# Candidates of two statistics in one four-bank PSUM tile, and paired VectorE word steps, in a four-layer graph kernel on one Trainium2 core

## The chip, the core and the metric

The kernel runs on one core of a Trainium2 chip. The metric is device time in microseconds for one execution of the whole program. In this text PE is TensorE (its weight loads are PEld), DVE is VectorE, ACT is ScalarE, POOL is GpSimd and SP is the engine that issues most transfers. L1151 is line 1151 of the kernel.

## The reference

Inputs are `x` (16 batches, 1024 nodes, 64 channels), a symmetric 0/1 matrix `adj` (16, 1024, 1024) with some 6% ones, and a node mask. Four layers follow one another, each as `x = x + layer(h)` with `h = max(layernorm(x), 0)`. Layer 0 is the costly one and the one that is changed. It takes, for every node and every channel, three quantiles over the node's neighbours, after some neighbours have been dropped:

```python
vals = jnp.where(nd[..., None], x[:, None, :, :], jnp.inf)     # nd: kept neighbours
s = jnp.sort(vals, axis=2)
nv = nd.sum(2)
for tau, w in zip((0.25, 0.5, 0.75), (0.25, 0.5, 0.25)):
    pos = tau * max(nv - 1, 0)
    lo, hi, frac = floor(pos), ceil(pos), pos - floor(pos)
    agg = agg + w * (v_lo + frac * (v_hi - v_lo))              # s at lo and at hi
out = x + agg
y = relu(out @ W1 + b1) @ W2 + b2
```

Layers 1 to 3 are a gated message passing, a small tanh network on `adj @ h`, and an attention with a softmax over columns; each multiplies a 1024x1024 matrix by node features.

## The kernel before

**No sort by neighbour list.** The kernel sorts each channel once over all 1024 nodes and then finds each node's quantiles by counting. `sort_pair` sorts the 128 channel rows of two batches at a time with a network of 55 compare steps on DVE. Forward, a step is three instructions: the comparison (L729, kept in DRAM as a mask), the maximum (L736) and the minimum (L737); each step needs the one before. Backward, the masks are loaded again and the positions are carried back through the same steps (L753, L754, then L760, or L756 and L757), which gives every node its rank as a code of a word (11 ranks) and a bit within it.

**Counting by matmul.** `neighbours` builds the kept-neighbour matrix `ndT` of a batch (scans on DVE at L825, transposes and sums on PE). `weights` turns codes into fp8 one-hot words, `wt`. `select` then handles one batch in four groups of two 128-node tiles (`TG = 2`), with these parts for each group:

- `words`: matmuls of `ndT` with `wt` (L1043) into PSUM tiles `comb` (four banks, four tiles), whose results ACT writes as 16-bit words `y` (L1051). PE transposes them (L1096) and ACT makes the sign matrices `sign` from them (L1098).
- `lasts`: on DVE, a tree of maxima over `y` (L1109, L1114, L1116 to L1125) that leaves in `z`, for each channel, the word in which the wanted rank lies. `y` has 36 rows of words, 32 called `full` and 4 called `rest`.
- `places`: some 26 16-bit bit operations on `z` (L966, L968, L971), which give four masks that say at which of the 12 lanes of the word the wanted value lies: `f2`, `f1`, `f`, `e0`.
- `values`: matmuls of `sign` with a table of value differences `vtab` (L1143) give, for every channel, the 12 candidate values of the word. Four copies under the four masks (L1151) move the wanted lane to lane 11, and `add_to` (L1018 the first time, L1020 after) adds it, times a coefficient, to `agg`.

There are two statistics (the median, and the two outer quantiles together, index `n`) and two signs (`sec`), so four candidates tiles for each 128-node tile, each `[P, 2, 512]` in two banks with channels halved over `e`. The pool `sc` has two buffers, so four banks; `comb` has the other four. The matmuls of one statistic number 40 (`n` = 0) or 32 (`n` = 1).

**Order.** Batches go in eight pairs. For a pair, `select` runs twice (with `compact` for rare nodes that need another way), then `extras` for those rare nodes of both batches (L1251 to L1317, with its own calls of `places` and of `pick`, the latter at L1011), then `layers` for both, up to the last addition at L1530. The neighbours and the sort of later pairs stand in the same part of the source, but a tile framework with a list scheduler writes the order on each engine: instructions without dependence are moved in between, by its own estimates, within what pools and buffers allow. So DVE's sort steps of the next pair fill places in `select`, `extras` and `layers` of the current one. Each engine then works strictly in that order and waits on semaphores.

```python
for i in range(2):
    wt, positive = weights(pr * 2 + i, kn, None if i else taken)
    select(pr * 2 + i, i, wt, positive, *made[i], aggs[i], kept, sw, sg, sy, sc, sp)
taken = extras(pr, kept, aggs, xs, xp)
for i, (ly, lb) in enumerate(((ly0, lb0), (ly1, lb1))):
    layers(pr * 2 + i, (pr * 2 + i) % 4, aggs[i], ly, lb)
if pr + 1 < pairs:
    made = prepare(pr + 1, nb, nbp)
    sort_pair(pr + 1, cur, sop)
```

Of the kernel before, what the change touches and what calls it, by code (L numbers as in the profile page):

```python
# [9 lines left out]
F32 = mybir.dt.float32  # L10
# [13 lines left out]
P = 128  # L24
# [18 lines left out]
def gnn_stack(ctx, tc, x, adj, nodemask, w, out):  # L43
# [915 lines left out]
    def places(sw, z, nf, kept=2):  # L959

        def word(name, bufs=1):
            return sw.tile([P, nf], U16, name=name, bufs=bufs)

        def bits(dst, src, v0, o0, v1=None, o1=None):
            if v1 is None:
                nc.vector.tensor_single_scalar(dst, src, v0, op=o0)  # L966
            else:
                nc.vector.tensor_scalar(dst, src, v0, v1, op0=o0, op1=o1)  # L968

        def both(dst, p, q, op):  # L970
            nc.vector.tensor_tensor(dst, p, q, op=op)  # L971

        zf = z.rearrange("p t s c -> p (t s c)")
        m, r, a, s0, s1, u1, u2 = (word(f"w_{n}") for n in ("m", "r", "a", "s0", "s1", "u1", "u2"))
        f1, f2, f, e0 = (word(f"w_{n}", kept) for n in ("f1", "f2", "f", "e0"))
        bits(m, zf, 1, SHL, 0xFFE, AND)
        bits(r, zf, 11, SHR, 31, XOR)
        bits(s0, m, 1, SHR, 0x555, AND)
        both(a, m, s0, ALU.subtract)
        bits(s0, a, 2, SHR, 0x333, AND)  # L980
        bits(s1, a, 0x333, AND)
        both(s1, s0, s1, ALU.add)
        bits(s0, s1, 8, SHR)
        bits(s1, s1, 4, SHR, 15, AND)
        both(s1, s1, s0, ALU.add)
        both(u1.bitcast(I16), r, s0, ALU.subtract)
        both(u2.bitcast(I16), r, s1, ALU.subtract)
        both(r, r, u1, ALU.min)
        both(r, r, u2, ALU.min)
        bits(f1, u1, 13, SHR, 4, AND)  # L990
        bits(f2, u2, 13, SHR, 4, AND)
        both(s0, f1, f2, ALU.add)
        both(m, m, s0, SHR)
        both(a, a, s0, SHR)
        bits(s1, a, 2, SHR, 3, AND)
        both(u1.bitcast(I16), r, s1, ALU.subtract)
        both(r, r, u1, ALU.min)
        bits(f, u1, 14, SHR, 2, AND)
        both(m, m, f, SHR)
        bits(s0, m, 1, SHR, 1, AND)  # L1000
        both(e0, s0, r, ALU.is_gt)
        return [v.rearrange("p (t s c) -> p t s c", t=z.shape[1], s=z.shape[2]) for v in (f2, f1, f, e0)]
# [13 lines left out]
    def add_to(ag, first, v, c):  # L1016
        if first:
            nc.vector.tensor_scalar(ag, v, c, None, op0=ALU.mult)  # L1018
        else:
            nc.vector.scalar_tensor_tensor(ag, v, c, ag, op0=ALU.mult, op1=ALU.add)  # L1020
# [7 lines left out]
    def select(b, i, wt, positive, ndT, row10, qb, qz, agg, kept, sw, sg, sy, sc, sp):  # L1028
        coef = row10[:, :, 3:9].rearrange("p t (k s) -> p t k s", s=2)
        if True:  # L1030
# [74 lines left out]
            def lasts(ys):  # L1105

                z = sw.tile([P, TG, 4, C], U16, name="z", bufs=2)
                for tl, y in enumerate(ys):
                    nc.vector.tensor_scalar_add(y[:, 1], y[:, 0], 2048.0)  # L1109

                    yu = y.bitcast(U16)
                    full, rest = yu[:, :, : 2 * NQ], yu[:, :, 2 * NQ :]
                    for v, n in ((full, 64), (full, 32), (full, 16), (full, 8), (rest, 64), (rest, 32), (rest, 16)):
                        nc.vector.tensor_tensor(v[:, :, :, :n], v[:, :, :, :n], v[:, :, :, n : 2 * n], op=ALU.max)  # L1114
                    zs = z[:, tl].rearrange("p (s k) c -> p s k c", k=2)
                    nc.vector.tensor_tensor(  # L1116
                        zs[:, :, 1, :].rearrange("p s (q d) -> p s q d", d=4), full[:, :, NQ:, :4], full[:, :, NQ:, 4:8],
                        op=ALU.max,
                    )
                    nc.vector.tensor_tensor(full[:, :, :NQ, :4], full[:, :, :NQ, :4], full[:, :, :NQ, 4:8], op=ALU.max)  # L1120
                    for s in range(2):
                        nc.vector.tensor_tensor(
                            zs[:, s, 0, :].rearrange("p (m q d) -> p m q d", m=4, d=4),
                            full[:, s, :NQ, :4].rearrange("p (m q) d -> p m q d", m=4),
                            rest[:, s, :, :16].rearrange("p m (q d) -> p m q d", d=4), op=ALU.max,  # L1125
                        )
                return z

            def values(g, signs, marks):
                for tl in range(TG):  # L1130
                    t = g * TG + tl
                    for s in range(4):
                        sec, n = divmod(s, 2)
                        cand = sc.tile([P, 2, 512], F32, name="cand")
                        for e in range(2):

                            terms = [(n * NQ + q, n, q, 4, (q % 8) * 48) for q in range(8 * e, 8 * e + 8)]
                            if n == 0:
                                terms += [(2 * NQ + m, 2, m, 16, (m % 2) * 192) for m in range(2 * e, 2 * e + 2)]
                            for i_, (chunk, part, q, d_, at) in enumerate(terms):  # L1140
                                tab = vtab[:, part].rearrange("p (q d l) -> p q d l", d=d_, l=24)
                                for half_ in range(2):
                                    nc.tensor.matmul(  # L1143
                                        cand[:, e, at : at + 12 * d_].rearrange("p (d l) -> p d l", l=12),
                                        signs[tl][sec][:, chunk, :], tab[:, q, :, half_ * 12 : half_ * 12 + 12],
                                        start=(i_ == 0 and half_ == 0), stop=(i_ == len(terms) - 1 and half_ == 1),
                                    )
                        v = cand[:, :, :384].rearrange("p e (c l) -> p e c l", l=12)
                        for (dst, frm, k), mk in zip(PICKS[1:], marks):
                            mk = mk[:, tl, s, :].rearrange("p (e c o) -> p e c o", e=2, o=1)  # L1150
                            nc.vector.copy_predicated(  # L1151
                                v[:, :, :, dst : dst + k], mk.to_broadcast([P, 2, C // 2, k]), v[:, :, :, frm : frm + k]
                            )
                        add_to(
                            agg[:, t, :].rearrange("p (e c) -> p e c", e=2), s == 0, v[:, :, :, 11],
                            coef[:, t, STATS[n], sec : sec + 1],
                        )

            nf = TG * 4 * C
            now = words(0)  # L1160
# [405 lines left out]
    for pr in range(pairs):  # L1566
        with tc.tile_pool(reuse_waits="tile", name="keep", bufs=1) as keep:
# [5 lines left out]
            with tc.tile_pool(reuse_waits="tile", name="kn", bufs=1) as kn:  # L1573
                with (
# [1 line left out]
                    tc.tile_pool(reuse_waits="tile", name="sw", bufs=1) as sw,  # L1576
                    tc.tile_pool(reuse_waits="tile", name="sg", bufs=2) as sg,
                    tc.tile_pool(reuse_waits="tile", name="sp", bufs=4, space=PSUM) as sp,
                    tc.tile_pool(reuse_waits="tile", name="sc", bufs=2, space=PSUM) as sc,
                ):  # L1580
                    for i in range(2):
                        wt, positive = weights(pr * 2 + i, kn, None if i else taken)
# [66 lines left out]
```

## Time and profile before

| | |
|---|---|
| three runs | 5937.49, 5952.29, 5957.01 us (median 5952.29) |
| the profiled execution | 5945.84 us, of which the span of its instructions is 5944.1 |
| mean granted TensorE clock | 0.838 |
| DVE busy | 5122.3 us (86%), 13031 instructions |
| PE busy | 4397.4 us (74%), 45010 matmuls |
| ACT busy | 3817.2 us (64%) |
| `values` matmuls, L1143 | 669.3 us |
| `values` copies, L1151 | 2048 instructions; the groups of 256, 128 and 64 elements took 420.1, 150.3 and 108.6 us |
| tree, L1114 | 672.1 us, 896 instructions |

A group's row gives busy time, the mean time of one instruction, and the idle time of its engine just before it with what ended that. Consecutive instructions of DVE overlap in these durations, so the sum of durations is more than the time they take. All shares are over the whole span, which has stages with different limits.

### The profile page before, as it was taken

The page shows a single profiled execution, that of the slowest core. Times are in us where ns is not written, and L with a number is a line of the kernel's source. Part 1 is how long each engine was busy: PE and PEld are TensorE (multiplying, and loading weights), DVE is VectorE, ACT ScalarE, POOL GpSimd, SP SyncE. Part 2 cuts the span into 40 slices and gives each one's busy share as a digit, 9 for nine tenths or more (in the row PEclk, how much of TensorE's full clock was granted, in tenths as well). Part 3 has the DMA queues.
Part 4 walks back from the last instruction along what each step waited for, and adds up shares of the span by engine and source line. Part 5 has one row for each costly group of instructions (what it writes and reads, how often), then busy time and mean ns, then how long its engine had stood idle before and what let it go on. Part 6 is the DMA issues. An engine that isn't in the chain of part 4 may idle for free. (4 is left out here: it accounts for less than half of the span.)

```text
span 5944.1 us, 114264 instructions
## 1 busy us (share of the span) xinstructions
PE 4397.4 (74%) x45010; PEld 2736.4 (46%) x45010; DVE 5122.3 (86%) x13031; ACT 3817.2 (64%) x5701; POOL 181.7 (3%) x283
## 2 busy tenths in 40 slices
PE   1488677895768858788577885788767886779856
PEld 1355443554435544355434554345443554436542
DVE  9999888998789987999879997798879999567744
ACT  2587647775576855668567665676566776577824
POOL 2000000000000000000000000000000000000000
PEclk5699778997889978899688996899868998789967
DMA  3401364014631146211561115611345013520024
GB/s 126 123 26 37 97 200 127 30 48 120 194 94 34 38 127 212 77 36 44 152 204 55 50 51 150 190 39 48 90 141 172 34 48 97 183 87 19 10 75 139
DMA packets 524419, 568.22 MB, mean 96 GB/s; under 512 B 263808, under 2 KB 413568, under 8 KB 523872
## 3 DMA queue, kind: packets, MB, share of 16 engines
q1 hardware_dynamic: 381472, 476.43, 26.3%
q10 hardware_dynamic: 140064, 81.84, 4.5%
q8 instruction: 355, 5.82, 0.4%
q0 software_dynamic: 2336, 2.57, 0.2%
q14 instruction: 192, 1.57, 0.1%
HBM read 376.95 MB, written 183.76 MB: 94 GB/s over the span
## 5 line engine op out<-in xcount | busy, mean ns | idle before, releaser
L1043 PE MATMUL comb<-wt,ndT 128*128 128x512 fp8e5 x6144 | 1442.3, 387 | 146.7 <-ACT sign L1098 121.7
L1051 ACT ACTIVATE y<-comb,qb 128x512 int16<-128x512 f32 x1152 | 744.1, 718 | 512.4 <-PE comb L1043 510.7
L1043 PEld LDWEIGHTS <-ndT 128*128 128x128 fp8e5 x6144 | 592.5, 99 | 876.8 <-issue 246.3
L1143 PE MATMUL cand<-vtab,sign 128*128 128x48 f16 (+1 forms) x18432 | 669.3, 191 | 54.0 <-DVE agg L1018 36.1
L1143 PEld LDWEIGHTS <-sign 128*128 128x128 fp8e5 x18432 | 645.2, 96 | 111.9 <-issue 51.8
L1098 ACT ACTIVATE sign<-comb,lower 128x1024 fp8e5<-128x1024 int16 (+1 forms) x640 | 696.5, 1088 | 0.0
L1098 ACT ACTIVATE sign<-comb,half 128x1024 fp8e5<-128x1024 int16 (+1 forms) x640 | 691.3, 1080 | 0.0
L1114 DVE TENSOR_TENSOR y<-y 128x512 uint16<-128x512 uint16 (+5 forms) x896 | 672.1, 792 | 8.4 <-PE comb L1096 7.2
L1151 DVE COPY_PREDICATED cand<-w_f,cand 128x256 f32<-128x256 uint16 (+1 forms) x1536 | 535.8, 383 | 75.0 <-PE cand L1143 72.8
L1096 PE MATMUL comb<-ident_b,y 128*128 128x128 bf16 x4608 | 316.9, 222 | 117.2 <-ACT sign L1098 76.8
L833 ACT COPY at<-pk 128x512 f32<-128x512 f32 x256 | 147.5, 586 | 384.5 <-PE pk L831 197.1
L1406 PE MATMUL bank<-adjT,nd 128*64 128x512 f32 x1024 | 307.4, 668 | 90.4 <-DMA adjT<-a_d 88.9
L1096 PEld LDWEIGHTS <-y 128*128 128x128 bf16 x4608 | 292.7, 99 | 145.5 <-issue 144.4
L875 PE MATMUL pk<-minus_b,rem 128*128 128x128 bf16 x1024 | 225.5, 247 | 175.2 <-ACT rem L856 175.1
L1406 PE MATMUL bank<-att,hs 128*64 128x512 f32 x512 | 211.0, 941 | 185.0 <-ACT hs L1522 185.0
L825 DVE TENSOR_TENSOR_SCAN cum<-ni 128x1024 f16<-128x1024 fp8e5 x128 | 295.0, 2306 | 32.6 <-POOL ni L821 23.2
L875 PE MATMUL pk<-ident_b,ni 128*128 128x128 bf16 x1024 | 223.3, 244 | 125.1 <-ACT ndT L881 62.7
L729 DVE TENSOR_TENSOR swapped<-s 128x512 uint16<-128x512 f32 x440 | 302.5, 687 | 5.8 <-ACT s L717 1.6
L737 DVE TENSOR_TENSOR s<-s 128x512 f32<-128x512 f32 (+2 forms) x440 | 289.8, 659 | 0.0
L736 DVE TENSOR_TENSOR s<-s 128x512 f32<-128x512 f32 (+2 forms) x440 | 289.6, 658 | 0.0
L921 DVE TENSOR_SCALAR wt<-node 128x2048 uint8<-128x2048 f16 x224 | 268.0, 1221 | 13.1 <-PE comb L1234 13.0
L831 PE MATMUL pk<-ident,a 128*128 128x128 f32 x1024 | 193.5, 339 | 112.9 <-DMA a<-in_adj_dram 79.8
(323 smaller groups left out, 8258.8 us busy)
## 6 DMA issues: line engine op xcount, KB each, us to landing
adjT<-a_d SPq DMA_DIRECT2D x384, 512.0 KB
a<-in_adj_dram SPq DMA_DIRECT2D x128, 512.0 KB
a_d<-at ACTq DMA_DIRECT2D x256, 256.0 KB
m_d<-swapped SPq DMA_DIRECT2D x104, 512.0 KB
swapped<-m_d SPq DMA_DIRECT2D x104, 512.0 KB
n_d<-nat SPq DMA_DIRECT2D x128, 128.0 KB
x_d<-xr SPq DMA_DIRECT2D x48, 256.0 KB
comb_x<-x_d ACTq DMA_DIRECT2D x24, 512.0 KB
```

What stands on the lines that cost most here:

```text
L729: nc.vector.tensor_tensor(side(swapped[:, k, :], j), hi, lo, op=ALU.is_gt)
L737: nc.vector.tensor_tensor(to_hi, lo, hi, op=ALU.min)
L825: nc.vector.tensor_tensor_scan(cum[:, t - t0, :], ni[:, t, :], wide[:, t, pad - 1 : pad - 1 + N], 0.0, op0=ALU.add, op1=ALU.add)
L875: nc.tensor.matmul(pk[:, n % 4, :], lhs, rhs, start=(n % 4 == 0 and m == 0), stop=(m == len(terms) - 1 and last),)
L1043: nc.tensor.matmul(pw, ndT[:, j, t * P : (t + 1) * P], wt[1 + g8][:, j].rearrange("p w c -> p (w c)"), start=(j == 0), stop=(j == NT - 1),)
L1051: nc.scalar.activation(y[:, 0, chunks, at : at + 8 * d_].rearrange("p q (w d) -> p q w d", d=d_), pw.rearrange("p (w q d) -> p q w d", w=8 ...
L1096: nc.tensor.transpose(pt[:, q - q0, :], y[:, 0, q, :].bitcast(BF16), ident_b)
L1098: nc.scalar.activation(signs[tl][s][:, q0:q1, :], pt.bitcast(I16), AF.Sign, bias=before[s], scale=-1.0, saturate=False,)
L1114: nc.vector.tensor_tensor(v[:, :, :, :n], v[:, :, :, :n], v[:, :, :, n : 2 * n], op=ALU.max)
L1143: nc.tensor.matmul(cand[:, e, at : at + 12 * d_].rearrange("p (d l) -> p d l", l=12), signs[tl][sec][:, chunk, :], tab[:, q, :, half_ * 12 ...
L1151: nc.vector.copy_predicated(v[:, :, :, dst : dst + k], mk.to_broadcast([P, 2, C // 2, k]), v[:, :, :, frm : frm + k])
L1406: nc.tensor.matmul(po[to : to + C, :], lhs, rhs[:, f * HALF : (f + 1) * HALF], start=(j == 0), stop=(j == NT - 1))
```

## The change

The two statistics of one sign now share one candidates tile `[P, 4, 512]` of four banks, and the pool has one buffer. 72 matmuls fill it; each of the four masked copies takes both statistics in one instruction of twice the size, with the mask read for both; the two additions to `agg` stay. The first three halvings of the tree take `full` and `rest` together. In `places`, words that get the same operation lie side by side in one tile, and three pairs of instructions become three instructions of twice the size, two of them reading one operand twice through a broadcast. `extras` calls the changed `places`. The matmuls, the elements that are handled and the results are the same.

```diff
--- before.py
+++ after.py
@@ -970,9 +970,17 @@
         def both(dst, p, q, op):
             nc.vector.tensor_tensor(dst, p, q, op=op)
 
+        def two(name, bufs=1):
+            return sw.tile([P, 2, nf], U16, name=name, bufs=bufs)
+
+        def twice_(v):
+            return v.rearrange("p (o n) -> p o n", o=1).to_broadcast([P, 2, nf])
+
         zf = z.rearrange("p t s c -> p (t s c)")
-        m, r, a, s0, s1, u1, u2 = (word(f"w_{n}") for n in ("m", "r", "a", "s0", "s1", "u1", "u2"))
-        f1, f2, f, e0 = (word(f"w_{n}", kept) for n in ("f1", "f2", "f", "e0"))
+        r = word("w_r")
+        ma, ss, uu, ff = two("w_ma"), two("w_s"), two("w_u"), two("w_ff", kept)
+        m, a, s0, s1, u1, u2, f1, f2 = (v[:, k, :] for v in (ma, ss, uu, ff) for k in range(2))
+        f, e0 = (word(f"w_{n}", kept) for n in ("f", "e0"))
         bits(m, zf, 1, SHL, 0xFFE, AND)
         bits(r, zf, 11, SHR, 31, XOR)
         bits(s0, m, 1, SHR, 0x555, AND)
@@ -983,15 +991,12 @@
         bits(s0, s1, 8, SHR)
         bits(s1, s1, 4, SHR, 15, AND)
         both(s1, s1, s0, ALU.add)
-        both(u1.bitcast(I16), r, s0, ALU.subtract)
-        both(u2.bitcast(I16), r, s1, ALU.subtract)
+        both(uu.bitcast(I16), twice_(r), ss, ALU.subtract)
         both(r, r, u1, ALU.min)
         both(r, r, u2, ALU.min)
-        bits(f1, u1, 13, SHR, 4, AND)
-        bits(f2, u2, 13, SHR, 4, AND)
+        bits(ff, uu, 13, SHR, 4, AND)
         both(s0, f1, f2, ALU.add)
-        both(m, m, s0, SHR)
-        both(a, a, s0, SHR)
+        both(ma, ma, twice_(s0), SHR)
         bits(s1, a, 2, SHR, 3, AND)
         both(u1.bitcast(I16), r, s1, ALU.subtract)
         both(r, r, u1, ALU.min)
@@ -1110,7 +1115,7 @@
 
                     yu = y.bitcast(U16)
                     full, rest = yu[:, :, : 2 * NQ], yu[:, :, 2 * NQ :]
-                    for v, n in ((full, 64), (full, 32), (full, 16), (full, 8), (rest, 64), (rest, 32), (rest, 16)):
+                    for v, n in ((yu, 64), (yu, 32), (yu, 16), (full, 8)):
                         nc.vector.tensor_tensor(v[:, :, :, :n], v[:, :, :, :n], v[:, :, :, n : 2 * n], op=ALU.max)
                     zs = z[:, tl].rearrange("p (s k) c -> p s k c", k=2)
                     nc.vector.tensor_tensor(
@@ -1129,11 +1134,10 @@
             def values(g, signs, marks):
                 for tl in range(TG):
                     t = g * TG + tl
-                    for s in range(4):
-                        sec, n = divmod(s, 2)
-                        cand = sc.tile([P, 2, 512], F32, name="cand")
-                        for e in range(2):
-
+                    for sec in range(2):
+                        cand = sc.tile([P, 4, 512], F32, name="cand")
+                        for ne in range(4):
+                            n, e = divmod(ne, 2)
                             terms = [(n * NQ + q, n, q, 4, (q % 8) * 48) for q in range(8 * e, 8 * e + 8)]
                             if n == 0:
                                 terms += [(2 * NQ + m, 2, m, 16, (m % 2) * 192) for m in range(2 * e, 2 * e + 2)]
@@ -1141,20 +1145,21 @@
                                 tab = vtab[:, part].rearrange("p (q d l) -> p q d l", d=d_, l=24)
                                 for half_ in range(2):
                                     nc.tensor.matmul(
-                                        cand[:, e, at : at + 12 * d_].rearrange("p (d l) -> p d l", l=12),
+                                        cand[:, ne, at : at + 12 * d_].rearrange("p (d l) -> p d l", l=12),
                                         signs[tl][sec][:, chunk, :], tab[:, q, :, half_ * 12 : half_ * 12 + 12],
                                         start=(i_ == 0 and half_ == 0), stop=(i_ == len(terms) - 1 and half_ == 1),
                                     )
                         v = cand[:, :, :384].rearrange("p e (c l) -> p e c l", l=12)
                         for (dst, frm, k), mk in zip(PICKS[1:], marks):
-                            mk = mk[:, tl, s, :].rearrange("p (e c o) -> p e c o", e=2, o=1)
+                            mk = mk[:, tl, 2 * sec : 2 * sec + 2, :].rearrange("p n (e c o) -> p (n e) c o", e=2, o=1)
                             nc.vector.copy_predicated(
-                                v[:, :, :, dst : dst + k], mk.to_broadcast([P, 2, C // 2, k]), v[:, :, :, frm : frm + k]
+                                v[:, :, :, dst : dst + k], mk.to_broadcast([P, 4, C // 2, k]), v[:, :, :, frm : frm + k]
                             )
-                        add_to(
-                            agg[:, t, :].rearrange("p (e c) -> p e c", e=2), s == 0, v[:, :, :, 11],
-                            coef[:, t, STATS[n], sec : sec + 1],
-                        )
+                        for n in range(2):
+                            add_to(
+                                agg[:, t, :].rearrange("p (e c) -> p e c", e=2), sec == 0 and n == 0,
+                                v[:, 2 * n : 2 * n + 2, :, 11], coef[:, t, STATS[n], sec : sec + 1],
+                            )
 
             nf = TG * 4 * C
             now = words(0)
@@ -1576,7 +1581,7 @@
                     tc.tile_pool(reuse_waits="tile", name="sw", bufs=1) as sw,
                     tc.tile_pool(reuse_waits="tile", name="sg", bufs=2) as sg,
                     tc.tile_pool(reuse_waits="tile", name="sp", bufs=4, space=PSUM) as sp,
-                    tc.tile_pool(reuse_waits="tile", name="sc", bufs=2, space=PSUM) as sc,
+                    tc.tile_pool(reuse_waits="tile", name="sc", bufs=1, space=PSUM) as sc,
                 ):
                     for i in range(2):
                         wt, positive = weights(pr * 2 + i, kn, None if i else taken)
```

## The prediction

> **What bounds the kernel now.** I read the page first, then windows cut at the kernel's own stages, then the groups of the touched lines with shapes apart, the timeline of DVE, and the waits.
>
> ```profile
> PE 4397.4 (74%) x45010; PEld 2736.4 (46%) x45010; DVE 5122.3 (86%) x13031; ACT 3817.2 (64%) x5701; POOL 181.7 (3%) x283
> ```
>
> DVE is the busiest engine, but 86% is an average. A pair of batches passes four stages, which I cut by DVE: *select* (first copy of L1151 to last addition into agg), *extras* (to L1315), *layers* (to the last L1530) and *run-up* (to the next pair's first copy). Rows: pair 2 (four rows), pair 6's extras and layers, pair 7's select and extras. Columns: length, busy us and instructions of PE, PEld, DVE, ACT, POOL, granted clock.
>
> ```profile
> 1778.60:2136.80 358.20, 302.69 (x3741) 199.46 (x3740) 336.86 (x891) 241.80 (x396) 4.21 (x7) 0.93 0.17 51
> 2136.80:2246.10 109.30, 57.30 (x793) 49.49 (x793) 98.02 (x211) 67.25 (x73) 8.60 (x13) 0.64 0.51 142
> 2246.10:2462.70 216.60, 157.94 (x798) 73.74 (x798) 177.26 (x471) 131.36 (x188) 5.56 (x8) 0.78 0.53 165
> 2462.70:2502.50 39.80, 33.20 (x298) 19.86 (x297) 39.56 (x79) 38.34 (x61) 0.00 (x0) 0.97 0.16 57
> 5007.50:5104.40 96.90, 53.38 (x782) 45.84 (x782) 82.33 (x182) 65.06 (x69) 6.28 (x11) 0.65 0.40 110
> 5104.40:5315.40 211.00, 157.68 (x804) 73.28 (x804) 124.91 (x340) 128.66 (x185) 5.97 (x10) 0.80 0.51 161
> 5344.60:5676.10 331.50, 294.53 (x3779) 195.12 (x3777) 252.78 (x716) 243.85 (x398) 2.03 (x2) 0.96 0.09 23
> 5676.10:5753.60 77.50, 30.00 (x464) 28.05 (x464) 43.92 (x95) 21.10 (x9) 0.32 (x2) 0.50 0.15 40
> ```
>
> Select, while there is sorting to mix in, is DVE's (21 us idle of 358), as is the run-up. Layers is not: 52 us less DVE work (pair 2 to pair 6) shortened it by 5.6. Extras is half and half: from pair 6 to pair 7 it lost 38.4 us of DVE work and 19.4 of length. In pair 7 nothing is left to sort, and select is a chain through PE, ACT and DVE (79 us of DVE idle). So what DVE saves counts by where it is saved.
>
> **Prices.** Groups of L1151 by shape, and DVE's timeline (start, duration):
>
> ```profile
> L1151 DVE COPY_PREDICATED cand<-w_f,cand 128x256 f32<-128x256 uint16 x1024 | 420.1, 427 | 74.7 <-PE cand L1143 72.8
> L1151 DVE COPY_PREDICATED cand<-w_f,cand 128x128 f32<-128x128 uint16 x512 | 150.3, 295 | 0.3
> L1151 DVE COPY_PREDICATED cand<-w_e,cand 128x64 f32<-128x64 uint16 x512 | 108.6, 226 | 0.4
> ```
> ```profile
> 1753.69 0.69 DVE L737 TENSOR_TENSOR s<-s 128x512 f32<-128x512 f32 x1
> 1754.41 0.69 DVE L729 TENSOR_TENSOR swapped<-s 128x512 uint16<-128x512 f32 x1
> 1755.02 0.69 DVE L736 TENSOR_TENSOR s<-s 128x512 f32<-128x512 f32 x1
> ...
> 1791.95 0.22 DVE L1151 COPY_PREDICATED cand<-w_e,cand 128x64 f32<-128x64 uint16 x1
> 1792.08 0.29 DVE L1151 COPY_PREDICATED cand<-w_f,cand 128x128 f32<-128x128 uint16 x1
> 1792.28 0.28 DVE L1020 SCALAR_TENSOR_TENSOR agg<-cand,row,agg 128x64 f32<-128x64 f32 x1
> ```
>
> An instruction overlaps the next by 0.08 us, so the price is start to start: 0.13 for 64 elements, 0.20 for 128, thus some 1.04 ns an element and 0.066 fixed. On SBUF words the tree's halvings give the same (128x4096 2.20, 128x512 0.335: 0.067 fixed). Second price: L729 needs the result of the L737 directly before it and starts 0.72 after it, where L736 follows L729 after 0.61. I put a *tight* pair, one that waits for its direct predecessor, at 0.12.
>
> **What is removed.** Copies: 2048 become 1024. Tree: 3 instructions fewer in each of 128 tiles, 384. Places: 3 fewer in 64 calls and 8 of extras, 216. All elements remain, so 1624 x 0.067 = 109 us of DVE.
>
> The paired word steps read one operand twice through a stride of zero. L760 does that already (128x1024 in 738 ns as a mean, against 685 for L1114 at 128x1024), so I keep the 2-byte rate; without it 144 instructions, 128 of them of 1024 elements, go from 0.60 to 1.13: +75.
>
> **What the order gives back.** The built programs, which hold an order and no time, show tight instructions on DVE rising from 954 to 1522: two picks that ran side by side on two tiles are now one dependent row, and the tree is one chain. 568 x 0.12 = 68 us. Net: DVE 41 us less.
>
> In the Trainium skill, Perfetto Trace Analysis (Optimizing Scalar/DVE Operations) puts the fixed cost at about 60 ns on SBUF and 125 on PSUM; the SBUF figure agrees, the copies on PSUM show 66. By the page the 1024 copies would save 128 us instead of 68, and the total would be 60 lower; the row decides.
>
> **The single buffer.** The first matmul of a tile now waits for the last addition of the one before, with all of PE's queue behind it; the first copy waits for all 72 matmuls, not 40.
>
> ```profile
> 5361.36 2.43 PE L1143 MATMUL cand<-vtab,sign 128*128 128x48 f16 x72
> ...
> 5363.02 1.55 DVE L1151 COPY_PREDICATED cand<-w_f,cand 128x256 f32<-128x256 uint16 x4 [1.59 <-PE cand L1143]
> ```
>
> [...] In the new order, other DVE work by the rows above fills that gap: the middle value in pairs 0 to 6 is 3.4 to 3.6 us, and shortfalls against 2.9 sum to 0.1 to 4 us a pair, where the trace lost 5 to 12 a pair on this wait (72.8 in all, 27 in pair 7). In pair 7, 17 refills have nothing between, but PE has 15 matmuls of L1043 (3.2 us) after most fills, and DVE was idle there anyhow. I take 0 for this term; bounds are -50 (the wait is gone in pairs 0 to 6) and +110 (half a microsecond at each of 224 refills, since PE, 303 busy of 358, can be late).
>
> The same page (Optimizing Tensor Performance, Matmuls) speaks against the edit: independent groups should rotate through banks so that one's evacuation overlaps the next one's matmuls. Taken literally each of 256 refills shows its 2.43 us, +620; the trace's DVE had other work to put there.
>
> **What is moved.** To fill those gaps the scheduler pulls the sort's way back (L753 to L760, "back") out of extras into select. DVE instructions a pair, mean of pairs 1 to 5, before to after:
> - select: forward sort 86 to 55, back 77 to 174, neighbours 6 to 20, rest 724 to 532, tight 18 to 61
> - extras: back 68 to 0, neighbours 49 to 30, rest 94 to 90, tight 18 to 56
> - layers: forward 57 to 68, back 30 to 1, neighbours 37 to 42, tight 35 to 19
> - run-up: forward 35 to 44
>
> Priced at 0.60 (forward), 0.40 (back: 130 of 512 elements at 0.335 and 45 of 1024 at 0.60; neighbours alike), 0.067 and 0.12:
> - select -18.6 + 38.8 + 5.6 - 12.9 + 5.2 = +18, at the same idle: +18 of length.
> - extras -27.2 - 7.6 = -35 of work. On the line from pair 6 (82.3 busy, 96.9 long) to pair 7 (43.9, 77.5), 63 busy is 87 long: -22, not -35.
> - layers 6.6 - 11.6 + 2 - 1.9 = -5 of work, -2 of length. Run-up +5.
> Sum -1 a pair, -5 for five. Pair 0: select gets 84 back instructions (+34) and 15 neighbour ones (+6), loses 6 forward (-4) and 186 others (-12), tight +3: +26; extras +2; layers loses 22 of work, -3 of length; run-up +4: +29. Pair 6: select +17, extras 84 instead of 96.9: +4. Pair 7: tight 127 to 306 (+21) against -13 in a stage with idle: +4 (0 to +20). Before pair 0, six more sort steps: +4.
>
> Total -5 + 29 + 4 + 4 + 4 = **+36 us** on the profiled execution (5945.8, of which the span is 5944.1): 5982. The runs' median, 5952.3, is 6 above that execution: **5988**.
>
> **Rivals.**
> - *The saving arrives* (0.28). Extras follows its DVE work (-13 more in six pairs, -78) and select's wait for candidates falls to what the order shows (-40): 36 - 118 = -82; half of both, -23. For: DVE is busy 98 of 109 us in extras. Against: pair 7's extras, 77.5 long with 43.9 busy. 5870 to 5929.
> - *The refill shows* (0.25). PE reaches a refill late, DVE eats its 3.4 us and stands; +110, about 6095. It decides from 0.2 us a refill on. For: the first group of a batch has more PE than DVE work between candidates (25 us against 13). Against: later groups have less.
> - *The paired steps lose the 2-byte rate* (0.05): +75.
> - *The forecast* (0.42): -10 to +75, from extras at either end.
>
> **Numbers.** About 18 us (0.3%) is what a measurement can tell from no change. The forecast gives slower 0.26, same 0.12, faster 0.04; the refill and the lost rate give slower 0.29, same 0.01; the saving gives faster 0.26, same 0.02. Slower 0.55, same 0.15, faster 0.30. The range, 5890 to 6085, takes in most of the saving and of the refill; the forecast alone is 5942 to 6027.
>
> **What would show it.** Right: select of pairs 1 to 5 near 375, extras near 87, layers unchanged, L760 mostly inside select, copies of 128x512 at 0.60 start to start, waits of copies for candidates near 75. Wrong: extras under 80, select under 365, that wait above 150, or paired steps of 128x1024 above 0.75 us.

## The result and the profile after

The changed kernel takes 6089.35 us (median of four runs, 6085.26 to 6097.96) against 5946.28 for the kernel before in the same session: a ratio of 1.0242, 95% interval 1.0219 to 1.0265, or +143 us. The forecast was 5988, its range 5890 to 6085. The profiled execution took 6085.26 us, span 6083.5, so +139 against the profiled execution of before, and the following is made against that.

The page's row of busy times:

```profile
PE 4476.2 (74%) x45010; PEld 2790.5 (46%) x45010; DVE 5060.8 (83%) x11407; ACT 3812.5 (63%) x5689; POOL 186.2 (3%) x283
```

DVE has lost the 1624 instructions and is 61.5 us less busy, and the program is 139 us longer. The stages, cut as in the prediction: pair 2 (four rows), pair 6's extras and layers, pair 7's select and extras; columns as there.

```profile
1812.90:2200.10 387.20, 309.48 (x3727) 205.78 (x3725) 351.08 (x779) 248.04 (x400) 5.66 (x10) 0.89 0.20 57
2200.10:2285.50 85.40, 48.54 (x769) 42.12 (x769) 60.24 (x120) 55.93 (x60) 5.44 (x8) 0.74 0.34 91
2285.50:2504.80 219.30, 161.42 (x816) 77.07 (x817) 170.14 (x440) 128.06 (x187) 9.46 (x10) 0.78 0.56 175
2504.80:2550.10 45.30, 39.07 (x322) 22.54 (x321) 45.02 (x78) 43.84 (x68) 0.00 (x0) 0.96 0.17 59
5133.90:5219.80 85.90, 51.87 (x773) 45.88 (x773) 58.93 (x114) 57.00 (x60) 3.14 (x8) 0.69 0.34 88
5219.80:5424.20 204.40, 152.71 (x804) 70.91 (x805) 125.95 (x341) 128.74 (x185) 7.77 (x10) 0.82 0.52 166
5455.30:5816.90 361.60, 302.91 (x3771) 200.81 (x3768) 256.44 (x525) 242.98 (x396) 2.03 (x2) 0.93 0.08 23
5816.90:5893.00 76.10, 30.01 (x464) 28.05 (x464) 42.47 (x92) 21.10 (x9) 0.32 (x2) 0.50 0.14 35
```

Select of pair 2 is 29 us longer with 112 instructions fewer on DVE; extras is 24 shorter. Pair 7's select, which has no sorting to mix in, is 30 longer although DVE has 191 instructions fewer there. Summed over all pairs, in us:

| stage | length before | after | DVE idle before | after | change of length | forecast |
|---|---|---|---|---|---|---|
| select | 2826.6 | 3063.9 | 219.1 | 318.9 | +237 | +137 |
| extras | 829.4 | 709.4 | 121.4 | 200.7 | -120 | -121 |
| layers | 1671.1 | 1656.4 | 439.8 | 460.0 | -15 | -13 |
| run-up | 267.6 | 300.5 | 12.8 | 14.7 | +33 | +29 |
| before pair 0 | 341.9 | 345.7 | | | +4 | +4 |

So the miss is in one place: 100 us of DVE's idle time in select. The groups of the copies, shapes apart (busy us, mean ns, then DVE's idle time just before them), show 62 of it (gaps over 60 ns inside select add up to 74.1 before and 135.8 after); another 15 are gaps under 60 ns (9 before, 24 after):

```profile
L1155 DVE COPY_PREDICATED cand<-w_ff,cand 128x512 f32<-128x512 uint16 x512 | 352.5, 688 | 137.2 <-PE cand L1147 133.4 <-PE comb L1200 2.3
L1155 DVE COPY_PREDICATED cand<-w_f,cand 128x256 f32<-128x256 uint16 x256 | 107.8, 421 | 1.3
L1155 DVE COPY_PREDICATED cand<-w_e,cand 128x128 f32<-128x128 uint16 x256 | 73.7, 288 | 1.5
```

How it looks in pair 7's select: PE's timeline, then DVE's (start, duration, and in brackets the idle time before):

```profile
5513.53 2.43 PE L1147 MATMUL cand<-vtab,sign 128*128 128x48 f16 x72
5515.81 3.40 PE L1048 MATMUL comb<-wt,ndT 128*128 128x512 fp8e5 x15
5519.04 2.43 PE L1147 MATMUL cand<-vtab,sign 128*128 128x48 f16 x72
```
```profile
5512.75 0.60 DVE L1025 SCALAR_TENSOR_TENSOR agg<-cand,row,agg 128x64 f32<-128x64 f32 x2
5516.00 1.43 DVE L1155 COPY_PREDICATED cand<-w_ff,cand 128x512 f32<-128x512 uint16 x2 [2.65 <-PE cand L1147]
5517.46 0.43 DVE L1155 COPY_PREDICATED cand<-w_f,cand 128x256 f32<-128x256 uint16 x1
5517.92 0.29 DVE L1155 COPY_PREDICATED cand<-w_e,cand 128x128 f32<-128x128 uint16 x1
5518.25 0.28 DVE L1023 TENSOR_SCALAR agg<-cand,row 128x64 f32<-128x64 f32 x1
5518.57 0.28 DVE L1025 SCALAR_TENSOR_TENSOR agg<-cand,row,agg 128x64 f32<-128x64 f32 x1
5521.51 0.69 DVE L1155 COPY_PREDICATED cand<-w_ff,cand 128x512 f32<-128x512 uint16 x1 [2.65 <-PE cand L1147]
```

The two engines take turns. The last addition ends at 5513.35, 0.18 later PE starts the fill, 0.04 after its end DVE copies, and 2.86 us later the tile is free again. A turn is 0.18 + 2.43 + 0.04 + 2.86 = 5.51 us. With two tiles the same two statistics of one sign followed each other at 4.43 in the kernel before (fills from 5395.84 and 5400.27, 10 word matmuls between). PE does not stand in the gap: 15 matmuls of `words` run there, 0.216 us apart, and the next fill starts 0.216 after the last of them. So the 0.18 is PE finishing `words` (where it stood idle for the tile, a fill began 0.05 after the addition, the median of 92 waits), and the 1.08 us by which the turn is longer are five more of these matmuls. They are the next group's, taken early, and at the head of that group PE then waits for ACT. PE's waits in pair 7's select:

```profile
PE comb L1048 <- ACT sign L1103: 13.6, 12, 1.6
PE comb L1101 <- ACT sign L1103: 10.1, 14, 1.3
...
PE cand L1147 <- DVE agg L1025: 6.6, 4, 3.0
```

PE's direct wait for DVE is as small as before (6.7), its waits at these two lines for `sign` were 4.1 and 2.5. One group of this select, from the transposes of its last word rows (x4 of L1101) to those of the next, went from 38.92 us to 42.35; times eight that is 27 of pair 7's 30 (an estimate: the first and last groups of a batch run otherwise). By PE's account the 30 us are 22 of idle time and 8 more of busy time, at a granted clock of 0.93 instead of 0.96. The two waits for `sign` make 23.7 here; with the single tile alone they are 8.9, with the tree alone 14.4 (*Pair 7 by parts*, below).

### The profile page after: what moved, and what is told of

It is laid out like the page before. It is cut to its first block, busy times and chain, and to the rows that moved or that the text cites. A ratio compares the mean times of both kernels' runs of the same rounds, so it can differ in the third digit from the quotient of the medians.

```text
span 6083.5 us, 112589 instructions
## 1 busy us (share of the span) xinstructions
PE 4476.2 (74%) x45010; PEld 2790.5 (46%) x45010; DVE 5060.8 (83%) x11407; ACT 3812.5 (63%) x5689; POOL 186.2 (3%) x283
## 3 DMA queue, kind: packets, MB, share of 16 engines
q1 hardware_dynamic: 381472, 476.43, 25.8%
## 5 line engine op out<-in xcount | busy, mean ns | idle before, releaser
L1147 PE MATMUL cand<-vtab,sign 128*128 128x48 f16 (+1 forms) x18432 | 719.7, 198 | 150.2 <-DVE agg L1025 121.7
L1147 PEld LDWEIGHTS <-sign 128*128 128x128 fp8e5 x18432 | 698.1, 101 | 232.8 <-issue 142.4
L1119 DVE TENSOR_TENSOR y<-y 128x4608 uint16<-128x4608 uint16 (+3 forms) x512 | 648.0, 1266 | 34.3 <-PE comb L1101 33.0
L1155 DVE COPY_PREDICATED cand<-w_ff,cand 128x512 f32<-128x512 uint16 x512 | 352.5, 688 | 137.2 <-PE cand L1147 133.4
L1101 PE MATMUL comb<-ident_b,y 128*128 128x128 bf16 x4608 | 316.1, 222 | 149.9 <-ACT sign L1103 121.1
L1101 PEld LDWEIGHTS <-y 128*128 128x128 bf16 x4608 | 288.4, 99 | 177.1 <-issue 176.2
```

The costliest lines, as they stand in the source:

```text
L1101: nc.tensor.transpose(pt[:, q - q0, :], y[:, 0, q, :].bitcast(BF16), ident_b)
L1147: nc.tensor.matmul(cand[:, ne, at : at + 12 * d_].rearrange("p (d l) -> p d l", l=12), signs[tl][sec][:, chunk, :], tab[:, q, :, half_ * 1 ...
L1155: nc.vector.copy_predicated(v[:, :, :, dst : dst + k], mk.to_broadcast([P, 4, C // 2, k]), v[:, :, :, frm : frm + k])
```

## Experiments

Theory A: the loss is the hand-over of the only tile. Each of 256 fills lies between a last addition and a first copy, and either DVE waits or other work must be put there. The main rival, B: the loss comes from DVE itself, its longer chains of dependent steps and the sort moved into select. The ratios are to the kernel before in the same session. "Busy" and "idle" are DVE's changes against the profile of before, summed over the four stages.

| run | what | ratio, interval | busy | idle | copies' wait |
|---|---|---|---|---|---|
| whole change | | 1.0242, 1.0219 to 1.0265 | -66 | +201 | 136 |
| e1 | single tile of four banks alone | 1.0107, 1.0080 to 1.0134 | -41 | +124 | 87 |
| e2 | tree and places, two tiles | 1.0022, 1.0008 to 1.0035 | -48 | +51 | 54 |
| e3 | before, one buffer | 1.0317, 1.0287 to 1.0347 | +32 | +163 | 153 |
| e4 | tree alone | 1.0023, 1.0008 to 1.0037 | -26 | +42 | 64 |
| e5 | places alone | 0.9975, 0.9959 to 0.9991 | -15 | +3 | 69 |
| e8 | single tile and tree | 1.0162, 1.0139 to 1.0184 | -53 | +124 | 98 |
| e9 | single tile and places | 1.0212, 1.0190 to 1.0235 | -44 | +162 | 98 |
| e6 | whole change, half fills | 0.9913, 0.9882 to 0.9944 | | | 109 |
| e7 | before, half fills | 0.9889, 0.9856 to 0.9922 | | | 96 |
| e11 | single tile alone, half fills | 0.9939, 0.9919 to 0.9959 | | | 107 |
| e10 | whole change, sort held back | 1.0294, 1.0257 to 1.0330 | -43 | +220 | 188 |

(before: 74. The half fills change what PE has to do, so busy and idle are left out there.)

**e1, the candidates alone.** The hunk of `values` and the pool, without tree and places:

```diff
-                        cand = sc.tile([P, 2, 512], F32, name="cand")
+                        cand = sc.tile([P, 4, 512], F32, name="cand")
...
-                    tc.tile_pool(reuse_waits="tile", name="sc", bufs=2, space=PSUM) as sc,
+                    tc.tile_pool(reuse_waits="tile", name="sc", bufs=1, space=PSUM) as sc,
```

> Only the candidates part of the change: one four-bank tile for both statistics, one buffer, copies of both at once; the tree and the places stay as before. DVE issues 1024 instructions fewer (-68 us at 0.067) and has 367 tight instructions more (+44 at 0.12), so by work alone about -24. Theory A (the single buffer costs idle time at the hand-over between PE and DVE, some 100 us, and makes the scheduler pull the sort into select): nearly all of the loss is here, +110 to +170 us, DVE idle before the copies 120 to 150 us against 75. Theory B (the loss comes from the longer dependent rows of the tree and the paired words): -30 to +30, idle before the copies near 75.

6018.22 us, +71: about half of the loss, with 41 us less work on DVE. Both theories miss: A had +110 to +170 and a wait of 120 to 150 us, B no more than +30. The copies' wait rose by only 13 us, while the scheduler put 164 of the sort's backward steps a pair into select (77 before); extras, left without them, stands idle for 83 us more.

**e2, tree and places on two tiles.**

```diff
-                    for v, n in ((full, 64), (full, 32), (full, 16), (full, 8), (rest, 64), (rest, 32), (rest, 16)):
+                    for v, n in ((yu, 64), (yu, 32), (yu, 16), (full, 8)):
...
-        both(u1.bitcast(I16), r, s0, ALU.subtract)
-        both(u2.bitcast(I16), r, s1, ALU.subtract)
+        both(uu.bitcast(I16), twice_(r), ss, ALU.subtract)
```

> Only the other two parts: the tree levels taken together and the paired word steps, with two two-bank buffers for the candidates as before. 600 DVE instructions fewer (-40 us) and tight instructions nearly as before (961 against 954), the sort where it was. Theory A: faster by 15 to 45 us, idle before the copies as before. Theory B: slower by 30 us or more; the L1114 tree and paired steps show gaps between their instructions.

5959.96 against 5947.11: 48 us of DVE work gone, 51 of idle time come, mostly in layers (440 to 506 idle). It neither gains nor costs as much as the theories said. The two parts account for 1.0107 and 1.0022; the whole costs 1.0242. Some 59 us (143 - 71 - 13; 67 by the ratios) arise only where they meet.

**e3, the kernel before with one buffer.**

```diff
-                    tc.tile_pool(reuse_waits="tile", name="sc", bufs=2, space=PSUM) as sc,
+                    tc.tile_pool(reuse_waits="tile", name="sc", bufs=1, space=PSUM) as sc,
```

> The kernel before with one edit: the candidates pool has one buffer of two banks in place of two. No instruction is merged and none removed. Theory A: slower, by 100 to 250 us, since each of 512 tiles is handed over alone; the sort's way back moves into select as in the changed kernel, extras gets short (near 88 us). Theory C (the four-bank merge itself is what makes the hand-over long, and a tile of two banks is refilled in 1.4 us, which other work hides): within 40 us of the kernel before, although 313 more tight instructions cost 38.

6144.48, +197, with no instruction added, removed or enlarged: inside theory A's range, far outside theory C's. In a middle pair 157 of the sort's backward steps lie in select, but extras of pair 2 is 97 us long, not 88. In the groups of DVE and PE (idle time last):

```profile
L1151 DVE COPY_PREDICATED cand<-w_f,cand 128x256 f32<-128x256 uint16 (+1 forms) x1536 | 578.4, 377 | 156.1 <-PE cand L1143 148.6 <-PE comb L1195 2.3
L1143 PE MATMUL cand<-vtab,sign 128*128 128x48 f16 (+1 forms) x18432 | 754.1, 198 | 205.1 <-DVE agg L1020 111.1 <-DVE agg L1018 70.6 <-DMA vtab<-w_d 15.4
```

The copies' 156.1 stood at 75.0 before, and the matmuls' 205.1 at 54.0. One edit, the same instructions, and the loss is larger than in the whole change: the second buffer is worth 197 us at 512 fills. Merging the statistics (e1) gives a part back: 73 us by DVE's busy time, which has half the copies, and 39 by idle time, with half the hand-overs.

**e4 and e5, tree and places each alone, on two tiles.** The first is the tree's line of e2's diff, the second all the rest of it.

> The seven tree steps of a packed tile as four (64, 32, 16 over all 36 columns of words, 8 over the 32 full ones), candidates as in the kernel before: two tiles of two banks. DVE has 12505 instructions, 992 of them wait for the instruction right before them (954 in the kernel before), so by the prices of the prediction its work falls by 384 x 0.067 - 38 x 0.12 = 21 us. Theory A (on two buffers DVE's saved time comes free as filler but the stages that it shares with PE and ScalarE only wait longer, as in the run with both DVE parts on two buffers, ratio 1.002): ratio 0.999 to 1.004, the wait of the first tree step for PE's comb (8.4 us before) up to about 25. Rival B (all of the DVE saving arrives when the paired word steps are left out; it is these that cost): ratio 0.996 or below. Rival C (the tree's merged levels cost by themselves, as each must wait for the rest of the words too): 1.006 or more.

> The three pairs of word steps of the places as one instruction each, tree and candidates as in the kernel before. DVE has 12673 instructions, 993 tight: 216 x 0.067 - 39 x 0.12 = 10 us less work. Theory A: ratio 0.999 to 1.004. Rival B (the paired word steps are what costs in the run with both parts): 1.004 or more here and below 0.997 with the tree alone.

5962.95 and 5932.36 against 5947.77. The tree alone is as theory A had it: 26 us less work, 42 more idle, and 24.5 us of wait ahead of its first step (8.4 before; up to 25 expected). The places alone are the only part that pays, by about what the count of instructions says (15 us, 10 expected), slightly more than theory A allowed. No rival holds: on two tiles neither part costs more than 15 us.

**e8 and e9, the single tile with one of the two.** e1 with the tree's line, and e1 with the places.

> Candidates in one tile of four banks and the tree of four steps; word steps of the places as before. DVE has 11481 instructions, 1477 tight. The candidates alone gave 1.0107, all three parts 1.0242, the other two without the candidates 1.0022: some 75 us come only when the parts meet. Theory A (each instruction saved brings DVE sooner to the refill of the only tile and makes the copies wait for PE, so the extra goes with the number of instructions saved, 384 of 600 by the tree): ratio 1.018 to 1.021, wait ahead of the copies 110 to 125 us (87 with the candidates alone, 136 in the whole change). Rival B (the places' pairs alone meet the single tile badly, through the chain of places to copies): ratio within 1.008 to 1.013. Rival C (the tree does it all): 1.023 or more.

> Candidates in one tile of four banks and the paired word steps; the tree of seven steps as before. DVE has 11649 instructions, 1430 tight. Theory A (extra in proportion to the instructions saved, 216 of 600): ratio 1.014 to 1.017, copies' wait 95 to 110 us. Rival B (the places' pairs do it all): 1.022 or more. Rival C (the tree does it all): 1.008 to 1.013.

6034.13 and 6065.56. Both add to e1 (+0.0055 and +0.0105), so no single part is to blame, but theory A's shares are wrong: the places with 216 instructions cost more than the tree with 384, close to rival B's 1.022. e8 lies in no theory's range. On two tiles the places gain 15 us, on the single one they lose 47 (medians) to 62 (ratios). Their loss lies in select of pairs 0 to 6, which sum to 2724 us (2683 in e1, 2674 in e8); I cannot say why. The order that the scheduler found around the fills differs in each run, and no run holds it fixed.

**e6 and e7, half fills.** The fill sums two addends of each table value; both kernels leave out the second, so half the matmuls of a fill, and the candidates lack that addend. The order changes with it: of the sort's backward steps 113 lie in a middle select in e6 and none in e7 (174 and 77 with full fills), so only pair 7, where nothing is left to sort, compares the fills alone.

```diff
-                                for half_ in range(2):
+                                for half_ in range(1):
```

> The changed kernel with half the matmuls that fill a candidate tile: the second of the two addends of the value table is left out. A four-bank tile takes 36 matmuls instead of 72, by the trace of the changed kernel 1.22 us instead of 2.43 from first to last; DVE does the same work on the same shapes. In the order as built, 113 instead of 174 of the sort's backward steps now lie in select. Theory A (the loss is the refill of the only tile: 24 refills a pair inside the groups of four tiles that DVE must wait through or cover): pair 7's select, where no sort can cover them, falls by 24 x 1.2 = 29 us from 361.6 to about 333, the wait ahead of its copies from 57.8 to about 30, a middle pair by 12 to 18 us, the whole to 5950 to 6000 us, ratio 1.001 to 1.010. Rival B (the loss is DVE's tight chains and the moved sort alone, PE's fill is covered): ratio 1.020 to 1.024, pair 7's select above 355.

> The control for the run beside it: the kernel before with the same half of the fill's matmuls left out. With two tiles the fill of the one runs while the other is used, so theory A expects little: ratio 0.990 to 1.000, pair 7's select from 331.5 to 320 to 331. If PE's load in select is what counts by itself, whatever the buffers (rival B), this falls as far as the run beside it: ratio 0.98 or below.

5903.66 and 5892.49. A fill of a four-bank tile now takes 1.29 us. Pair 7's select, windows of e6 and of e7:

```profile
5297.60:5627.90 330.30, 264.21 (x2655) 162.84 (x2652) 252.21 (x525) 242.38 (x396) 2.03 (x2) 0.92 0.09 24
```
```profile
5301.80:5620.80 319.00, 268.36 (x2664) 163.80 (x2661) 250.83 (x716) 243.65 (x398) 2.03 (x2) 0.93 0.09 23
```

The changed kernel's went from 361.6 to 330.3 (333 expected), the wait of its copies from 57.8 to 36.7 (30 expected); the kernel before gains 12.5 there. Of the 143 us between the two kernels 11 are left, and of the 30 in pair 7's select also 11. The whole fell further than theory A said (5950 to 6000), partly because PE's work in select counts by itself: the control lost 65 us, also a little more than expected. Most of the loss goes with the length of the fill. By rival B the changed kernel should have stayed at 1.020 or more; against its control it is at 1.002.

**e11, the single tile alone with half fills.** e1 with the same edit as e6; the candidates lack the second addend here too. It asks whether tree and places cost through the fills.

> Candidates in one tile of four banks alone (tree and places as before), and half the matmuls of its fill: the second addend of the value table is left out. What is open: with full fills the tree and the places' pairs added 71 us to the single tile (6089.4 against 6018.2), on two tiles only 13 (5960.0 against 5947.1). With half fills the whole change took 5903.7. As built, 34 of the sort's backward steps lie in select, 74 in extras. Theory A (the tree and the pairs cost only through the refills, since they bring DVE to them sooner): with half fills they add no more than about 15, so this run takes 5885 to 5910 us, ratio 0.988 to 0.993. Rival B (they cost through their own chains of dependent steps, whatever the refill takes): this run is some 70 us below the whole change with half fills, 5820 to 5845 us, ratio 0.977 to 0.982.

5921.61, ratio 0.9939, against 0.9913 with tree and places in e6. With half fills the two parts cost nothing that can be told (the intervals overlap); with full fills, on the same single tile, they cost 1.3%. The run is 12 us above theory A's window and over 75 above the rival's. So over the whole program most of their cost goes with the length of the fill; the order differs here too (34 backward steps in a middle select, 113 in e6).

**Pair 7 by parts.** With nothing left to sort, the last pair's select shows the parts without the moved sort. Lengths in us, and PE's waits for `sign` at the two lines shown above:

| tile and fill | neither | tree | places | both | `sign`: neither, tree, both |
|---|---|---|---|---|---|
| two tiles, full | 331.5 | 340.8 (e4) | 331.7 (e5) | 340.9 (e2) | 6.6, 14.4, 14.2 |
| single, full | 347.5 (e1) | 362.0 (e8) | 345.8 (e9) | 361.6 | 8.9, 23.7, 23.7 |
| two tiles, half | 318.9 (e7) | | | | 14.4 |
| single, half | 321.8 (e11) | | | 330.3 (e6) | 18.8, both 29.1 |

Of the 30 us, 16 come with the single tile, and with half fills 3 of these are left: this part goes with the length of the fill. The other 14 come with the tree; 9 of them come on two tiles too, and 8.5 with half fills, so in this stage the tree has a cost of its own, as rival C of e4 had it. Its merged first step writes over `rest` as well, and so cannot start before PE has transposed those last four rows. DVE's wait for it in pair 7's select, of the kernel before and of e4:

```profile
DVE y L1114 <- PE comb L1096: 4.3, 6, 0.7
```
```profile
DVE y L1114 <- PE comb L1096: 16.9, 8, 2.4
```

The places cost nothing in this stage. How the tree's wait lengthens the loop through PE and ACT is not shown.

**e10, the sort held back.** The second half of the sort's backward steps is held behind select's last addition:

```diff
+            if behind is not None and k0 < 28:
+                late.enter_context(tc.issue_after(behind))
+                behind = None
             swapped = so.tile([P, GROUP, N // 2], U16, name="swapped", bufs=2)
```

> The changed kernel with the second half of the sort's backward steps held behind the last instruction of select on DVE. Per middle pair 83 of the backward steps lie in select, 75 in extras, 17 in layers (the changed kernel: 174, 0, 1; the kernel before: 77, 68, 30); nothing else is changed. DVE has 1709 tight instructions instead of 1522. Rival B (what costs is that the sort's way back was moved into select: the extras then have nothing to cover their own waits): select falls by 91 x 0.40 = 36 us to about 350, extras grow by 22 to about 109, so 14 us a pair less, the whole near 5990, ratio 1.005 to 1.010. Theory A (the refills of the only tile must be covered by something, and the sort's steps were the cover): select falls by no more than 22 us and keeps more idle time (32 us now, 45 to 60 then), extras still grow by some 20, and the whole stays at 6075 to 6130 us, ratio 1.021 to 1.031.

6129.40, ratio 1.0294. Select and extras of pair 2:

```profile
1824.20:2198.60 374.40, 305.61 (x3727) 202.34 (x3725) 317.46 (x683) 239.89 (x392) 4.43 (x9) 0.90 0.17 49
2198.60:2304.50 105.90, 58.91 (x791) 51.28 (x792) 94.81 (x204) 65.42 (x70) 10.58 (x11) 0.63 0.47 131
```

Over pairs 1 to 5 select lost 33.8 us of DVE work, but only 10.8 of length (386.1 to 375.3), and its idle time went from 31.9 to 54.9; extras grew by 19.4. The wait in pair 2's select:

```profile
DVE cand L1161 <- PE cand L1153: 22.6, 12, 3.9
```

It was 15.2 with the sort there. That is theory A in each number. The moved sort accounts for 10.8 of the 28 us by which the change lengthened a middle select; for the rest it only stood in for DVE's wait.

## Why the prediction was wrong

- *Removed and tight, net -41 us of DVE.* DVE's busy time in the stages fell by 66. In select, gaps under 60 ns rose from 9 to 24 us; with these the fall is 51. So 568 more tight instructions cost 0.08 to 0.10 us each, not 0.12: right within 10 to 25 us, and on the good side.
- *Paired steps keep the 2-byte rate; copies of 128x512 at 0.60.* Both right. DVE's timeline has a copy 0.59 before a paired step of 1024 and that 0.61 before the next copy; the rival of the lost rate is out:

```profile
5540.06 0.69 DVE L1155 COPY_PREDICATED cand<-w_ff,cand 128x512 f32<-128x512 uint16 x1
5540.65 0.69 DVE L971 TENSOR_TENSOR w_ma<-w_ma,w_s 128x1024 uint16<-128x1024 uint16 x1
5541.26 0.69 DVE L1155 COPY_PREDICATED cand<-w_ff,cand 128x512 f32<-128x512 uint16 x1
```

- *What moves.* Right. Work in a middle select rose by 17.4 (18 forecast); L760 there went from 14 instructions to 45 in pair 2 and from 18 to none in extras; extras 87.5 us long (87), layers +1.0 (-2), run-up +5.2 (+5). (The sum for extras leaves out its 38 more tight instructions, +4.6 by the prediction's own price; the busy time came out at 62.0 all the same, 63 forecast.) The rival that the saving arrives fails with this. A middle select is 386 us long where the sign of being right was near 375, and the copies' wait 136 where it was near 75.
- *The single buffer at 0: the step that failed.* The prediction let select grow "at the same idle". Its idle time rose by 100 us: 73 in pairs 0 to 6 and 26.5 in pair 7. With the single tile alone it rose by 25 there and by 83 in extras, which lost its sort steps (e1); the other 75 in select come only with tree and places on it. Three things were wrong in the working. First, no run shows the 2.9 us against which the gaps were set. With hand-overs of 0.05 and 0.04 a refill is 2.5 us at full clock (2.65 where PE is still at `words`), so this was on the safe side; but where PE had stood idle before a fill, it ran at half the granted clock, as the next fence shows, and the refill took 4.1. Of the 192 fills that are not the first of a group of four, 45 took over 2.6 us; at most 31 us of the copies' waits go back to this (for each fill no more than what it took beyond 2.43). (In pairs 0 to 6, 49 of 224 tiles made DVE wait, 78 us in all; 33 of these lie at six first tiles of a group, where fill and `words` are interleaved over some 20 us.) Second, I took the middle gap (3.4 to 3.6 us) against 2.9 and a sum of shortfalls from an order without times; the trace lost 7 to 17 us on the copies' wait in pairs 1 to 5, not 0.1 to 4 (and pair 7 of the kernel before had lost 25.8, not 27). Third, pair 7: "DVE was idle there anyhow" is true and no reason. There a refill is on the loop through both engines, and the turn itself became longer (+28.5 in that pair, +4 forecast); the tree's wait for the last transposes, 9 to 14 us of it, was put at nothing.

Windows of L1147 alone (PE, PEld, granted clock, DMA share, GB/s), a fill that follows 1.9 us of waiting for DVE in pair 2, and the fill from pair 7 shown above:

```profile
2191.80:2195.80 4.00, 3.99 (x72) 3.75 (x71) 0.50 0.29 85
5513.53:5515.96 2.43, 2.43 (x72) 2.32 (x71) 1.00 0.03 7
```

The same 72 matmuls take 4.00 us instead of 2.43, and in pair 2 DVE waited 2.56 for them. The 43 fills that took 3.2 to 4.2 us had a median of 3.4 us of PE idle in the 4 us before them, the 147 under 2.6 us had 0.2. Of a fill's 72 matmuls 64 are 48 columns wide and 8 are 192 wide; they start 25 and 82 ns apart at full clock, 40 and 160 at half. In the kernel before 575 of the fills' 18432 matmuls came at the 40 ns, in e2 568 and in e5 514; with the single tile it is 2945 in the changed kernel, 2501 in e1 and 2949 in e3. At 15 ns each that is 36 us more of filling for the change; the wide ones (336 at 160 ns, 59 before) add 22. That is more than the 31 that can stand in the copies' waits, and it goes with the single buffer in every run: PE waits for the tile and is then slow to fill it. The Trainium skill (TensorE: Matmul & The Clock Gate, HAM oscillation) has this pattern for a wait on transfers: idle gaps of some 3.4 us put PE's clock to half, and the next burst pays. The trace agrees in part: 16 of the 43 slow fills had a single idle gap of 3.4 us or more in the 6 us before them, and the least idle time in those 4 us was 1.6. No run here keeps PE busy ahead of a fill, so what the clock costs in the end, beside the wait itself, stays open.

- *The rival that the refill shows.* It had the size (6095; measured 6089) and mostly the wrong cause, a late PE. The median refill of pairs 1 to 5 starts 0.06 us after the tile is free; in pairs 0 to 6, 36 of the 168 that are not the first of a group started over 0.5 us late, and 14 of the 45 us of waits at these 168 lie there. And the copies' wait in pairs 0 to 6, where it put its 110 us, rose by 30 (48 to 78). So the size is luck.
- *The page's rule on rotating banks* (Trainium skill, Perfetto Trace Analysis, Optimizing Tensor Performance, Matmuls) pointed the right way, and e3 shows it at 1.0317. Taken literally at +620 it is four times too much for the change: other work did hide most of each fill.

## What to carry to other kernels

Before a double-buffered tile becomes one tile twice the size, write down the loop: last use, fill, first use. If other work is to cover the fill, it is taken from a place where it covered something else, and it must be charged there; where nothing is left to move in (the last pair), the loop's full length is the price. To price a lost buffer, run the old kernel with one buffer less: one number in the source showed more here than the counting of gaps, though its 197 us are more than the 71 of the merged tile alone. And before two steps are merged, look what the merged one must wait for that the first of them did not.

## What the hardware showed beside that

- The fill is nearly all matmul rate: 72 matmuls 2.43 us, 36 matmuls 1.29, so 32 ns each as a mean (25 for 48 columns, 82 for 192) and 0.15 for the burst, although each record lasts 182 ns or more. The hand-over from DVE to a PE that waits and back took 0.05 and 0.04.
- Copies on PSUM cost the same from start to start as 16-bit steps on SBUF of twice the elements (0.59 for 512 f32, 0.61 for 1024 uint16).
- The mean granted clock does not order the runs: e6, the second fastest, had 0.807 (span 5899.9), e8 0.845 (6019.5). In one place it counts: the half-clock fills above, and the group of pair 7's select, where PE was 36.76 us busy at 1.00 before and 38.03 at 0.96 after.
